# Layer norm of two token blocks together: two column sums side by side in the TensorE array, results spread through DRAM

## The chip, the cores and the metric

The kernel runs on one core of a Trainium2 chip. The metric is the device time of one execution in microseconds (us). The kernel before takes 2467.66 us, the median of 4 runs (2467.39 to 2468.02).

## The reference

The program is a stack of four layers on a tensor x of 4 batches, 512 channels and 32 x 32 = 1024 tokens, all in float32. Layer 0 is an attention with 8 heads, layer 1 a linear attention, layer 2 a layer norm with an attention of one head, layer 3 a group norm with an attention of 4 heads. Each layer adds its result to x. The change lies in the norm of layer 2:

```python
xf = jnp.transpose(x, (0, 2, 3, 1)).reshape(b, h * w, c)      # c = 512
mu = jnp.mean(xf, axis=-1, keepdims=True)
var = jnp.var(xf, axis=-1, keepdims=True)
xn = (xf - mu) * jax.lax.rsqrt(var + 1e-5) * norm_w
qkv = jnp.einsum('bnc,dc->bnd', xn, w_qkv) + b_qkv
attn = softmax(einsum('bqc,bkc->bqk', q, k) * c ** (-0.5))
out = einsum('bqk,bkc->bqc', attn, v)
return x + out @ w_proj.T + b_proj                            # and back to b, c, h, w
```

## The kernel before

**Data.** A batch of x stays in SBUF for the whole program as `xs[b]`: 128 partitions, NC = 4 chunks of 128 channels, 1024 tokens. Tokens are worked on in NTB = 2 blocks of TB = 512. So a channel is a partition in one of four chunks, a token is a column, and a sum over the 512 channels of a token is a sum of four chunks and then a sum down the 128 partitions. The second part is done on TensorE, as a matmul with a matrix of ones. Names: `ones` is 128 x 128; `eps` holds 1e-5; `row` (L89) hands out tiles of 128 x 512, five of them in all; `block` (L85) hands out tiles of four chunks by 512, twelve in all; `tr_tile` hands out one of two PSUM banks for small sums and projections. `sc_tile` and `acc_tile` are the banks of the large products, two of each. All loads, and the writes to DRAM that matter here, are issued from SyncE (SP), in one queue.

**The norm.** `layer_norm(b, dst)` (L797) takes the two token blocks one after the other. For a block, `total` (L804) has VectorE add the four chunks into a tile `part` (L812), and TensorE multiply `part` by all of `ones` (L814): every one of the 128 output rows is the same sum, so the bank `lnsum` holds the total, already copied to each partition. VectorE then computes x - mean for the four chunks (L821), reading the bank; ScalarE squares them (L828); `total` is called a second time on the squares; ScalarE takes the square root of variance + eps (L834), VectorE the reciprocal (L835), and VectorE scales the four chunks by it and by the weight `nw2` (L838). That makes two totals a block, four a batch, 16 in all.

**The order of work.** A norm is a generator. It stands in a list `background`, and `slot()` (L159), which the product loops call between their groups of matmuls, advances it by one `yield`; `later(ticks, f)` (L169) defers a step by so many slots in the same manner, and `finish()` (L176) empties the list. The order so written is not the last word: a scheduler fixes the order of the instructions of each engine when the program is built. Each engine then works through its list in that order.

- Batch 0's norm is started by `start_norm` (L888, called at L924) ahead of layer 0's attention for the last batch, and its steps are placed among the groups of that attention. There a step of `Attention.scores` (L505) is two matmuls into the halves of a bank (L517), an exponential on ScalarE (L528) and, on VectorE, the running sum of the exponentials (L532 for the first, L536). `values` (L544) multiplies the exponentials by v (L554) and copies the result out (L562). After the steps of two heads the sums go to the softmax denominators, and the result, which stands in the tiles of q by then, is multiplied by their reciprocals `rb` (L598).
- Layer 2's loop (L1005) runs over the four batches. It begins with two large products of the normed input: `channels_first` (L1012) gives q, and `tokens_first` gives v, into which VectorE adds parts of products (L356). The products go through `two_by_sevens` (L297 to L320): seven block products in the place of eight, each two groups of matmuls (L312), with VectorE forming the differences of the factors and adding the parts up, and a `slot()` after each pair of groups. After `tokens_first` the next batch's norm is started (L1028), for b = 3 a group norm; so the norms of batches 1 to 3 run among the scores (put L1041, add L1045, exponential L1048) and the values of the batch before.
- Between scores and values of layer 2, VectorE forms the softmax sums `sum0` and `sum1` and the factors `t1` (L1078), `t2` (L1087) and `t4` (L1088). The results are put and added at L1097 and L1102; the addition to x (L1107) follows a multiplication by `rb` (L1105). Weights for the next batch are loaded by `load_folded` (L967, 1 MB a transfer).

**The form that sums of several columns already use.** `spread_reciprocals` (L453) takes up to four partial sums. Each is multiplied by 32 columns of `ones` (L460), so that its total appears on 32 of the 128 partitions of one bank, `den`: four such products occupy the four quarters of the array's columns. One reciprocal (L471) serves all of them. One row of each quarter is written to a tile in DRAM (L473), and `send` reads it back, repeated on all 128 partitions, into `rb` (L589 in layer 0, L1082 in layer 2) or `dens`. Layer 0's denominators and those of layer 2's softmax go this way. `check` (L449, L995) computes bounds for a range check; the fallback that hangs on it is not executed for these inputs.

Of the kernel before, what the change touches and what calls it, by code (L numbers as in the profile page):

```python
# [12 lines left out]
F32 = mybir.dt.float32  # L13
AF = mybir.ActivationFunctionType
ALU = mybir.AluOpType
AX = mybir.AxisListType

P = 128
B = 4
C = 512  # L20
S = 1024
NC = C // P
NT = S // P
TB = 512
NTB = S // TB
# [32 lines left out]
def conv_fast(ctx: ExitStack, tc: tile.TileContext, d: dict, out: bass.AP, flag):  # L58
# [5 lines left out]
    nc = tc.nc  # L64
# [3 lines left out]
    work = ctx.enter_context(tc.tile_pool(name="work", bufs=1))  # L68
    small = ctx.enter_context(tc.tile_pool(name="small", bufs=2))
    PSUM = bass.MemoryType.PSUM  # L70
    dram = ctx.enter_context(tc.tile_pool(name="dram", bufs=1, space=bass.MemoryType.DRAM))
# [10 lines left out]
    def tr_tile(name="tr"):  # L82
        return ps_tr.tile([P, TB], F32, tag="tr", name=name)

    def block(name):  # L85

        return work.tile([P, NC, TB], F32, tag="blk", bufs=12, name=name)

    def row(name):  # L89
        return work.tile([P, TB], F32, tag="row", bufs=5, name=name)  # L90
# [5 lines left out]
    xs = [xpool.tile([P, NC, S], F32, tag=f"x{b}", name=f"x{b}") for b in range(B)]  # L96
# [29 lines left out]
    ones = const.tile([P, P], F32, name="ones")  # L126
    nc.vector.memset(ones, 1.0)
    eps = const.tile([P, 1], F32, name="eps")
# [21 lines left out]
    def col(name, c):  # L150
        return cols[:, COL[name] + c : COL[name] + c + 1]
# [125 lines left out]
    def right(xb, tiles, over=False):  # L277


        b11, b21 = xb[0][:, :HC, :], xb[0][:, HC:, :]  # L280
        b12, b22 = xb[1][:, :HC, :], xb[1][:, HC:, :]
        tt = nc.vector.tensor_tensor
        t3, t2, t4 = (tiles[i]() for i in range(3))
        t1 = b12 if over else tiles[3]()
        tt(t3, b22, b12, ALU.subtract)
        tt(t1, b12, b11, ALU.subtract)
        tt(t2, b22, t1, ALU.subtract)
        tt(t4, b21, t2, ALU.subtract)
        return {1: b11, 2: b21, 3: b22, 4: t4, 5: t1, 6: t2, 7: t3}
# [160 lines left out]
            den, den, 0.0, r, ALU.add, ALU.add, accum_out=next_unit(den.partition_size())  # L450
        )

    def spread_reciprocals(sums, send, check):  # L453


        ps = tr_tile("den")
        Q = P // 4

        def product_of(j):
            return nc.tensor.matmul(  # L460
                ps[j * Q : (j + 1) * Q, :], lhsT=ones[:, :Q], rhs=sums[j], start=True, stop=True
            )


        first = product_of(len(sums) - 1)
        with tc.issue_after(first.ins):
            for j in range(len(sums) - 1):
                product_of(j)
        n = len(sums) * Q
        r = work.tile([P, TB], F32, tag="r", bufs=1, name="r")  # L470
        nc.vector.reciprocal(r[:n, :], ps[:n, :])  # L471
        row_of = dram.tile([4, TB], F32, tag="recip", bufs=2, name="recip")
        nc.sync.dma_start(row_of[: len(sums), :], r[:n:Q, :])  # L473
        send(row_of)
        check(ps[:n, :], r[:n, :])

    class Attention:

# [100 lines left out]
        def normalize_four(s, qb, gs, to):  # L579
            sums = [s.sums.pop((qb, g)) for g in gs]  # L580
            if s.pair:
                to = spare_tile("rb")
                sums = [t[:, half, :] for t in sums for half in range(2)]

            def send(rows):
                if s.pair:
                    for half in range(2):
                        p = slice(half * s.hd, (half + 1) * s.hd)
                        nc.sync.dma_start(to[p, :, :], rows[half::2, :].partition_broadcast(s.hd))  # L589
                else:  # L590
                    n = len(sums)
                    nc.sync.dma_start(to[:, :n, :], rows[:n, :].partition_broadcast(P))

            spread_reciprocals(sums, send, check_range)

            def multiply():
                o = s.q[qb][:, gs[0] : gs[-1] + 1, :]
                nc.vector.tensor_tensor(o, o, to[:, : len(gs), :], ALU.mult)  # L598
                if s.last and qb < NTB - 1:
                    later(1, lambda: s.project_out(qb))  # L600

            later(2 if s.by > 2 else 3, multiply)
# [193 lines left out]

    def layer_norm(b, dst):  # L797

        for tb in range(NTB):
            x = xs[b][:, :, bass.ts(tb, TB)]  # L800
            xn = block("ln")
            dst.append(xn)

            def total(of):  # L804

                part = row("part")
                for c in range(NC):
                    a = of(c)
                    if c == 0:
                        first = a  # L810
                    else:
                        nc.vector.tensor_tensor(part, first if c == 1 else part, a, ALU.add)  # L812
                ps = tr_tile("lnsum")
                nc.tensor.matmul(ps, lhsT=ones, rhs=part, start=True, stop=True)  # L814
                return ps

            yield
            mean = total(lambda c: x[:, c, :])
            yield
            for c in range(NC):  # L820
                nc.vector.scalar_tensor_tensor(  # L821
                    xn[:, c, :], mean, -1.0 / C, x[:, c, :], ALU.mult, ALU.add
                )
            yield

            def square(c):
                sq = row("sq")
                nc.scalar.activation(sq, xn[:, c, :], AF.Square)  # L828
                return sq

            var = total(square)
            yield
            rstd = row("rstd")
            nc.scalar.activation(rstd, var, AF.Sqrt, bias=eps, scale=1.0 / C)  # L834
            nc.vector.reciprocal(rstd, rstd)  # L835
            yield
            for c in range(NC):
                nc.vector.scalar_tensor_tensor(  # L838
                    xn[:, c, :], xn[:, c, :], col("nw2", c), rstd, ALU.mult, ALU.mult
                )  # L840
            yield

# [58 lines left out]
    for b in range(B):  # L901
        xb = [xs[b][:, :, bass.ts(tb, TB)] for tb in range(NTB)]
        if b == 0:
            q = first_q(w0[0], "bqkv0", xb)
            x = right(xb, [pt_tile] * 4)
# [17 lines left out]
        if b == B - 1:  # L923
            start_norm(layer_norm, 0, "ln0")  # L924
            rawk = load("rawk", d["wraw2"], 1)
            rawq = load("rawq", d["wraw2"], 0)
        else:
            loads.start("q")
        att = Attention(
            b, q, k, v, 8, None, eb, then=lambda b=b: linear_attention(b),  # L930
# [73 lines left out]
    scale = float(C) ** -0.5  # L1004
    for b in range(B):  # L1005
        xn = norms.pop(f"ln{b}")
        x = right(xn, [pt_tile] * 4)
# [19 lines left out]
        if b + 1 < B:  # L1027
            start_norm(layer_norm, b + 1, f"ln{b + 1}")  # L1028
        else:
            start_norm(group_norm, 0, "gn0")  # L1030
# [50 lines left out]
        def send(rows):  # L1081
            nc.sync.dma_start(rb, rows[:2, :].partition_broadcast(P))  # L1082

        later(1, lambda: spread_reciprocals([sum0[:, 0, :], sum1[:, 0, :]], send, check_spread))

        def last_factors():
# [49 lines left out]
    total = small.tile([P, 1], F32, tag="ks", name="total")  # L1136
    nc.vector.tensor_reduce(total, stat, AX.X, ALU.add)
    ps = tr_tile("flag")
# [484 lines left out]
```

## Time and profile before

| | us |
|---|---|
| median of 4 runs | 2467.66 |
| profiled execution | 2467.66 |
| its span (first to last instruction) | 2465.7 |
| TensorE busy (PE) | 2451.8 (99%) |
| TensorE weight loads (PEld, beside matmuls) | 1148.9 (47%) |
| VectorE busy (DVE) | 1429.2 (58%) |
| ScalarE busy (ACT) | 785.5 (32%) |
| GpSimd busy (POOL) | 2.1 |
| mean DMA rate | 55 GB/s |

The clock that TensorE was granted is 1.00 over the span. By stage, in us of the span:

| stretch | what runs | PE busy | DVE busy | ACT busy |
|---|---|---|---|---|
| 0 to 956 | layer 0, with layer 1 and batch 0's norm among it | 949.4 | 623.9 | 377.6 |
| 956 to 1003 | folding of layer 2's weights | 47.0 | 36.3 | 5.6 |
| 1003 to 1622 | layer 2, with the norms of batches 1 to 3 | 617.8 | 414.8 | 177.1 |
| 1622 to 2465.7 | layer 3 | 837.7 | 354.2 | 225.3 |

The groups of the norm (instructions, busy time, mean of one):

| line | engine | what | count | busy us | mean ns |
|---|---|---|---|---|---|
| L812 | DVE | adds of x, and of squares | 16 + 16 | 11.0 + 11.0 | 688 |
| L814 | PE | total, 128 x 128 by 128 x 512 | 32 | 16.8 | 605 |
| L821 | DVE | x - mean | 32 | 20.1 | 681 |
| L828 | ACT | squares | 32 | 18.9 | 627 |
| L834 | ACT | table load ahead of the square root | 8 | 10.3 | 1283 |
| L835 | DVE | reciprocal | 8 | 26.7 | 3340 |
| L838 | DVE | scaling | 32 | 22.4 | 743 |

How to read it: a float32 matmul of the program shows as two records, so L814's 16 totals are 32. The busy time of a group is less than count times mean where ends overlap, since matmuls are pipelined and their ends are modelled; the distance between the starts of two neighbours is what one of them costs the engine. A timeline line gives the start in us, the length of the group of like instructions, engine, line, operation, output and inputs; what stands in brackets at its end is idle time ahead of it, and what ended that. In the list of waits, the numbers after the colon are the idle us, how often, and the longest.

### The profile page before, as it was taken

To read this page: it belongs to the slowest core of one execution; us is meant where nothing else is said; L and a number is where in the kernel's file an instruction comes from. 1 tells how busy PE (TensorE), PEld (TensorE's weight loads), DVE (VectorE), ACT (ScalarE), POOL (GpSimd) and SP (SyncE) were. 2 spreads that over 40 slices of the span, in tenths; PEclk is the share of its full clock that TensorE was granted. 3 is DMA by queue.
4 is the path that set the end of the run, shared out by engine and by line. 5 is a ranking of instruction groups with operands and counts; after the bars stand their busy time and mean duration, and the time that the engine had idled before them with its cause. 6 is when DMAs were issued, how large, how long until landed. Compare 5 with 4: busy or idle time off the path is not lost.

```text
span 2465.7 us, 19958 instructions
## 1 busy us (share of the span) xinstructions
PE 2451.8 (99%) x7730; PEld 1148.9 (47%) x7730; DVE 1429.2 (58%) x1732; ACT 785.5 (32%) x1120; POOL 2.1 (0%) x12
## 2 busy tenths in 40 slices
PE   9999999999999999999999999999999999999999
PEld 4534543454345334554645546446446445544643
DVE  3576567656765887568587673733553443444344
ACT  1452345135513651342241412213312321331231
POOL 0000000000000000000000000000000000000000
PEclk9999999999999999999999999999999999999999
DMA  6203100310131003002112020210031022013001
GB/s 239 94 18 120 35 1 18 120 35 1 26 112 35 9 14 114 35 0 94 52 41 100 7 76 1 77 51 18 17 137 51 1 103 102 1 52 119 18 18 44
DMA packets 44224, 135.80 MB, mean 55 GB/s; under 512 B 3446, under 2 KB 3958, under 8 KB 36572
## 3 DMA queue, kind: packets, MB, share of 16 engines
q1 hardware_dynamic: 41820, 130.28, 15.3%
q10 hardware_dynamic: 2304, 4.20, 0.5%
q8 instruction: 62, 1.02, 0.2%
q14 instruction: 38, 0.31, 0.0%
HBM read 113.28 MB, written 21.18 MB: 55 GB/s over the span
## 4 chain that ended last, share of the span: by engine, by line
PE 97%; DVE 2%; ACT 0%; issue 0%; DMA 0%; SPq 0%; DVEq 0%
PE sc L312 30%; PE acc L312 22%; PE acc L554 18%; PE sc L517 16%; PE acc L517 2%; PE acc L206 1%; PE sc L206 1%; PE z L683 1%; PE den L460 1%; PE wval L786 1%; PE kx L729 1%; PE xtr L719 1%; PE po L206 1%; PE kv L206 1%; PE lnsum L814 0%; DVE sum L536 0%
## 5 line engine op out<-in xcount | busy, mean ns | idle before, releaser
L517 PE MATMUL sc<-q,k 64*128 64x512 f32 (+1 forms) x1284 | 421.6, 601 | 1.0 <-ACT ptt L528 0.8
L554 PE MATMUL acc<-ptt,v 128*64 128x512 f32 (+1 forms) x992 | 307.7, 598 | 0.0
L528 ACT ACTIVATE ptt<-sc 128x1024 f32<-128x1024 f32 x215 | 214.5, 1026 | 219.4 <-PE sc L517 219.1
L517 PEld LDWEIGHTS sc<-q,k 64*128 64x128 f32 (+1 forms) x1284 | 165.4, 188 | 231.2 <-issue 194.0
L536 DVE TENSOR_TENSOR sum<-sum,ptt 128x1024 f32<-128x1024 f32 x144 | 176.2, 1224 | 104.9 <-ACT ptt L528 97.3
L554 PEld LDWEIGHTS acc<-ptt,v 128*64 128x64 f32 (+1 forms) x992 | 107.9, 155 | 185.9 <-issue 184.8
L536 DVE TENSOR_TENSOR sum<-sum,p 128x1024 f32<-128x1024 f32 x112 | 137.1, 1224 | 61.5 <-ACT p L528 46.8
L554 PE MATMUL acc<-p,v 128*64 128x512 f32 (+1 forms) x544 | 159.5, 596 | 0.0
L528 ACT ACTIVATE p<-sc 128x1024 f32<-128x1024 f32 x106 | 106.8, 1037 | 95.4 <-PE sc L517 95.4
L352 ACT COPY v<-sc 128x256 f32<-128x256 f32 x144 | 53.6, 372 | 224.8 <-PE sc L312 222.6
L333 ACT ACTIVATE k<-sc,cols 128x512 f32<-128x512 f32 x48 | 33.0, 687 | 263.2 <-PE sc L312 263.2
L471 DVE RECIPROCAL r<-den 128x512 f32<-128x512 f32 (+1 forms) x28 | 94.0, 3356 | 36.8 <-PE den L460 36.3
L532 DVE TENSOR_TENSOR sum<-ptt 128x1024 f32<-128x1024 f32 x52 | 63.6, 1223 | 86.7 <-ACT ptt L528 77.8
L554 PEld LDWEIGHTS acc<-p,v 128*64 128x64 f32 (+1 forms) x544 | 56.1, 152 | 97.0 <-issue 97.0
L312 PE MATMUL acc<-ptt,ws 128*128 128x512 f32 x224 | 101.2, 592 | 0.0
L356 DVE TENSOR_TENSOR v<-acc,v 128x256 f32<-128x256 f32 x144 | 55.5, 418 | 68.2 <-PE acc L312 60.7
L562 ACT COPY q<-acc 128x512 f32<-128x512 f32 x64 | 37.6, 587 | 160.5 <-PE acc L554 160.5
L312 PE MATMUL sc<-ptt,w 128*128 128x512 f32 x168 | 75.5, 592 | 0.0
L337 DVE TENSOR_TENSOR k<-acc,k 128x512 f32<-128x512 f32 x48 | 31.6, 687 | 66.5 <-PE acc L312 66.5
L312 PEld LDWEIGHTS acc<-ptt,ws 128*128 128x128 f32 x224 | 42.3, 190 | 52.1 <-issue 52.1
L517 PE MATMUL acc<-q,k 64*128 64x512 f32 x252 | 66.1, 601 | 0.0
L333 ACT ACTIVATE q<-sc,cols 128x512 f32<-128x512 f32 x42 | 28.9, 688 | 109.1 <-PE sc L312 109.1
(356 smaller groups left out, 3481.4 us busy)
## 6 DMA issues: line engine op xcount, KB each, us to landing
ws<-kept SPq DMA_DIRECT2D x28, 1024.0 KB, 4.8
w<-in_wqkv SPq DMA_DIRECT2D x24, 1024.0 KB, 6.1
kept<-wsum SPq DMA_DIRECT2D x8, 1024.0 KB
rb<-recip SPq DMA_DIRECT2D x32, 256.0 KB, 4.1
w<-in_wo SPq DMA_DIRECT2D x7, 1024.0 KB, 5.9
dens<-recip SPq DMA_DIRECT2D x7, 1024.0 KB, 4.6
x<-in_x SPq DMA_DIRECT2D x3, 2048.0 KB
wqk<-kept SPq DMA_DIRECT2D x6, 1024.0 KB, 5.0
```

Of the source, the lines that this page charges most:

```text
L206: nc.tensor.matmul(ps, lhsT=lhs(c), rhs=rhs(c), start=(c == 0), stop=(c == NC - 1))
L312: nc.tensor.matmul(ps, lhsT=lhs, rhs=rhs, start=not more and j == 0, stop=(j == pieces - 1), skip_group_check=more,)
L333: nc.scalar.activation(out[at[1]][:, o, :], ps, AF.Identity, bias=bias(o))
L352: nc.scalar.copy(at_block(which, at), ps)
L356: nc.vector.tensor_tensor(c, ps, c, ALU.add)
L471: nc.vector.reciprocal(r[:n, :], ps[:n, :])
L517: nc.tensor.matmul(ps[half], lhsT=s.k[key // QT][p0:p1, g, bass.ts(key % QT, P)], rhs=s.q[qb][p0:p1, g, :], start=True, stop=True,)
L528: nc.scalar.activation(pt, pair_of, AF.Exp, scale=s.scale)
L532: nc.vector.tensor_tensor(t, s.pts[i - 1], pt, ALU.add)
L536: nc.vector.tensor_tensor(t, t, pt, ALU.add)
L554: nc.tensor.matmul(ps[p0:p1, :], lhsT=s.v[key // QT][:, key % QT, g * P + p0 : g * P + p1], rhs=pt[:, half, :], start=(key == 0), stop=(ke ...
L562: nc.scalar.copy(s.q[qb][:, g, :], s.accs.pop((qb, g)))
```

## The change

The norm handles both token blocks of a batch at once and takes over the form of `spread_reciprocals`, which is split into `column_totals` (the products into quarters) and `rows_of` (the write of one row of each quarter to DRAM). For each batch:

- VectorE adds up the chunks of both blocks into two tiles `part`. One `column_totals` of the two gives both sums, each on 32 partitions of one bank.
- ScalarE scales the bank by -1/C into a tile `total` of 64 partitions, two rows of it go to DRAM, and two transfers bring each row back, repeated on 128 partitions, as `lnrow` tiles: the negated means.
- After two `yield`s, VectorE adds the means to x, now a `tensor_tensor` of two SBUF tiles instead of a `scalar_tensor_tensor` that reads PSUM.
- Squares and their adds are as before. One `column_totals` gives both variances; one square root and one reciprocal on 64 partitions serve both blocks, and two rows go through DRAM to `lnrow` tiles in the same way.
- After two more `yield`s, VectorE scales all chunks of both blocks.

For a batch that makes two pairs of 128 x 32 products in the place of four 128 x 128 products, one table load, one square root and one reciprocal in the place of two each, one added scaling on ScalarE and six added transfers (two writes of two rows, four reads of 256 KB). The steps between the `yield`s are fewer and larger.

```diff
@@ -450,8 +450,7 @@
             den, den, 0.0, r, ALU.add, ALU.add, accum_out=next_unit(den.partition_size())
         )
 
-    def spread_reciprocals(sums, send, check):
-
+    def column_totals(sums):
 
         ps = tr_tile("den")
         Q = P // 4
@@ -466,13 +465,22 @@
         with tc.issue_after(first.ins):
             for j in range(len(sums) - 1):
                 product_of(j)
-        n = len(sums) * Q
-        r = work.tile([P, TB], F32, tag="r", bufs=1, name="r")
-        nc.vector.reciprocal(r[:n, :], ps[:n, :])
-        row_of = dram.tile([4, TB], F32, tag="recip", bufs=2, name="recip")
-        nc.sync.dma_start(row_of[: len(sums), :], r[:n:Q, :])
-        send(row_of)
-        check(ps[:n, :], r[:n, :])
+        return ps[: len(sums) * Q, :]
+
+    def rows_of(t):
+
+        n = t.partition_size()
+        rows = dram.tile([4, TB], F32, tag="recip", bufs=2, name="recip")
+        nc.sync.dma_start(rows[: n * 4 // P, :], t[:: P // 4, :])
+        return rows
+
+    def spread_reciprocals(sums, send, check):
+
+        ps = column_totals(sums)
+        r = work.tile([P, TB], F32, tag="r", bufs=1, name="r")[: ps.partition_size(), :]
+        nc.vector.reciprocal(r, ps)
+        send(rows_of(r))
+        check(ps, r)
 
     class Attention:
 
@@ -796,47 +804,65 @@
 
     def layer_norm(b, dst):
 
-        for tb in range(NTB):
-            x = xs[b][:, :, bass.ts(tb, TB)]
-            xn = block("ln")
-            dst.append(xn)
-
-            def total(of):
-
-                part = row("part")
-                for c in range(NC):
-                    a = of(c)
-                    if c == 0:
-                        first = a
-                    else:
-                        nc.vector.tensor_tensor(part, first if c == 1 else part, a, ALU.add)
-                ps = tr_tile("lnsum")
-                nc.tensor.matmul(ps, lhsT=ones, rhs=part, start=True, stop=True)
-                return ps
-
+
+        blocks = range(NTB)
+        xb = [xs[b][:, :, bass.ts(tb, TB)] for tb in blocks]
+        xn = [block("ln") for _ in blocks]
+        dst.extend(xn)
+
+        def partial(of):
+
+            part = row("part")
+            for c in range(NC):
+                a = of(c)
+                if c == 0:
+                    first = a
+                else:
+                    nc.vector.tensor_tensor(part, first if c == 1 else part, a, ALU.add)
+            return part
+
+        def spread(t):
+            rows = rows_of(t)
+            to = [row("lnrow") for _ in blocks]
+            for tb in blocks:
+                nc.sync.dma_start(to[tb], rows[tb : tb + 1, :].partition_broadcast(P))
+            return to
+
+        parts = []
+        for tb in blocks:
             yield
-            mean = total(lambda c: x[:, c, :])
+            parts.append(partial(lambda c: xb[tb][:, c, :]))
+        yield
+        ps = column_totals(parts)
+        t = row("total")[: ps.partition_size(), :]
+        nc.scalar.activation(t, ps, AF.Copy, scale=-1.0 / C)
+        mean = spread(t)
+        yield
+        yield
+        parts = []
+        for tb in blocks:
+            for c in range(NC):
+                nc.vector.tensor_tensor(xn[tb][:, c, :], mean[tb], xb[tb][:, c, :], ALU.add)
             yield
+
+            def square(c):
+                sq = row("sq")
+                nc.scalar.activation(sq, xn[tb][:, c, :], AF.Square)
+                return sq
+
+            parts.append(partial(square))
+            yield
+        ps = column_totals(parts)
+        t = row("total")[: ps.partition_size(), :]
+        nc.scalar.activation(t, ps, AF.Sqrt, bias=eps[: ps.partition_size(), :], scale=1.0 / C)
+        nc.vector.reciprocal(t, t)
+        rstd = spread(t)
+        yield
+        yield
+        for tb in blocks:
             for c in range(NC):
                 nc.vector.scalar_tensor_tensor(
-                    xn[:, c, :], mean, -1.0 / C, x[:, c, :], ALU.mult, ALU.add
-                )
-            yield
-
-            def square(c):
-                sq = row("sq")
-                nc.scalar.activation(sq, xn[:, c, :], AF.Square)
-                return sq
-
-            var = total(square)
-            yield
-            rstd = row("rstd")
-            nc.scalar.activation(rstd, var, AF.Sqrt, bias=eps, scale=1.0 / C)
-            nc.vector.reciprocal(rstd, rstd)
-            yield
-            for c in range(NC):
-                nc.vector.scalar_tensor_tensor(
-                    xn[:, c, :], xn[:, c, :], col("nw2", c), rstd, ALU.mult, ALU.mult
+                    xn[tb][:, c, :], xn[tb][:, c, :], col("nw2", c), rstd[tb], ALU.mult, ALU.mult
                 )
             yield
```

## The prediction

> **What bounds the kernel now.** I read the page, the waits of TensorE, and then timelines around the two kinds of column sum.
>
> ```profile
> PE 2451.8 (99%) x7730; PEld 1148.9 (47%) x7730; DVE 1429.2 (58%) x1732; ACT 785.5 (32%) x1120; POOL 2.1 (0%) x12
> PE sc L206 <- DMA wq<-in_wqkv: 5.7, 1, 5.7
> PE acc L312 <- DVE v L356: 0.9, 1, 0.9
> PE sc L517 <- ACT ptt L528: 0.8, 2, 0.6
> ```
>
> TensorE (PE) works for all of the span; its waits after the start come to 2 us. So time is won only where TensorE gets less work, and lost where another engine now makes it wait. Idle VectorE or ScalarE time is worth nothing by itself.
>
> The totals to be replaced, in layer 2 (start, length, records):
>
> ```profile
> 1074.71 3.60 PE L312 MATMUL acc<-q,ln 128*128 128x512 f32 x8
> 1078.15 1.02 PE L814 MATMUL lnsum<-part,ones 128*128 128x512 f32 x2
> 1079.01 3.60 PE L312 MATMUL sc<-rq,ptt 128*128 128x512 f32 x8
> ```
>
> A float32 matmul is two records 0.43 us apart. Starts count, since ends overlap: one total costs 1079.01 - 1078.15 = 0.86 us. The two-sum form exists already, for layer 2's softmax:
>
> ```profile
> 1133.94 1.88 PE L312 MATMUL acc<-p,v 128*128 128x512 f32 x4
> 1135.75 1.05 PE L460 MATMUL den<-sum,ones 128*32 128x512 f32 x4
> 1136.73 1.13 PE L312 MATMUL acc<-p,v 128*128 128x512 f32 x2
> 1137.69 0.59 PE L312 MATMUL sc<-t,sv 128*128 128x512 f32 x1
> ```
>
> Before it, four records fill TensorE to 1135.66; after it, two fill 0.86 ahead of 1137.69, from 1136.83. The pair costs 1.17 us, against 1.72 for two totals.
>
> What spreading through DRAM takes is seen in layer 0:
>
> ```profile
> 885.71 3.36 DVE L471 RECIPROCAL r<-den 128x512 f32<-128x512 f32 x1
> 889.10 0.53 SPq L473 DMA_DIRECT2D recip<-r  x1
> 890.87 1.24 SPq L589 DMA_DIRECT2D rb<-recip  x2
> 895.99 1.23 DVE L598 TENSOR_TENSOR q<-q,rb 128x1024 f32<-128x1024 f32 x1 [1.45 <-DMA rb<-recip]
> ```
>
> The reader may leave 1.77 us after the write; both 256 KB rows have landed 6.9 us after the write was issued. The second read leaves 0.65 later than the first; rb landings have a median of 4.0 us, so I take 5.9 us for the first row.
>
> The last view, ScalarE in layer 0's last attention, shows how norm work gets into the way of the softmax:
>
> ```profile
> 846.31 1.00 ACT L528 ACTIVATE ptt<-sc 128x1024 f32<-128x1024 f32 x1
> 847.22 1.14 ACT L828 ACTIVATE sq<-ln 128x512 f32<-128x512 f32 x2
> 848.26 1.01 ACT L528 ACTIVATE ptt<-sc 128x1024 f32<-128x1024 f32 x1
> 849.32 1.13 PE L517 MATMUL sc<-q,k 64*128 64x512 f32 x4 [0.58 <-ACT ptt L528]
> ```
>
> Squares stand between two exponentials, and TensorE, which needs the bank that the second one frees, waits.
>
> **What the Trainium skill says.** "TensorEngine Tiling (Array Packing)", Key Properties: tiles of the array work in parallel, but a change of mode drains it. The trace agrees: a pair costs 0.31 more than one total. "TensorE: Matmul & The Clock Gate", Architectural detail: ScalarE's and VectorE's queues are strict FIFO; the last view agrees. "DMA: Bandwidth & Descriptors", Anatomy of one DMA: about 2 us of a transfer is fixed, mostly the receipt of the write; 1.77 here. "ScalarE: Activation LUTs", What ACT_TABLE_LOAD costs: 1.28 us; the table loads at L834 take 1.28.
>
> **The change, part by part.** The profiled execution took 2467.66 us (span 2465.7 and 2.0 around it), the same as the median.
>
> (1) TensorE's work. Layer 2 computes the norms of batches 1 to 3: 12 totals x 0.86 = 10.3 become 6 pairs x 1.17 = 7.0: -3.3. Batch 0's norm runs in layer 0's last attention, where a total costs 1.05 (817.56 to 818.61): 4.2. Its first pair stands between attention groups: the four-sum den there costs 1.00 (884.58 to 885.58), two sums at least 0.88 and at most 1.17; I take 1.00. In the built order its second pair follows a softmax den in the same mode: two record steps of 0.44, 0.88. So -2.3.
>
> (2) Waits on `v`. Two first totals stand ahead of matmuls that wait for VectorE's adds (L356): 0.9 in the list, 0.2 in a gap (1354.8 to 1355.07). A pair that is 0.31 longer uses up 0.3 and 0.2 of them: -0.5 (bounds 0 and -1.1).
>
> (3) VectorE and ScalarE. 8 reciprocals of 3.34 become 4; 8 scalings by ScalarE stay 8 (0.69); 8 table loads go; the 32 subtractions keep 0.68 (L812's tensor_tensor: 0.69). This is hidden by TensorE before and after: 0, except in (4) and (5).
>
> (4) Batch 0: a new wait. VectorE's subtraction waits for the mean rows; behind it wait the running sums (L536). ScalarE's squares wait for the subtraction; behind those stand exponentials, and behind these TensorE. Put together from the rows: the value group ahead of the pair starts 1.05 + 0.4 earlier than 824.71 (the first total and a wait for its squares are gone), ends at 825.1; pair to 826.1; score and value groups (1.91, 1.87) follow, and the score group after two of each is due at 833.7. Sums are visible 1.13 after a pair's start (884.58 to 885.71): 826.3; scaling 0.69: 827.0; rows at 832.9 and 833.8. The first subtraction ends at 833.6. In the order built, two squares precede the exponential of the score group of 829.9: they run 833.7 to 834.9, the exponential to 835.9. The group due at 833.7 starts at 836.0: +2.3. Its second half waits for another square and exponential: +0.5. The second block's squares alternate with exponentials likewise, each behind subtractions (0.6) that stand among sums (1.13): the next two score groups get their second and first half 1.2 late each. Sum 5.2; the waits that today's squares cause at 822.4 and 847.6 go (groups of 2.31 and 2.77 for 1.91): -1.3. Net +3.9; bounds 0 (rows early) and 7 (rows 3 us later).
>
> (5) Layer 2: is there room? Clock from the variance pair's start. Sums visible 1.1, table load 1.28, square root 0.69, reciprocal 3.35, handovers: 6.6. Row at 12.5, second at 13.4. Eight scalings at 0.66: 17.8; four adds `p<-acc` (0.6): 20.2. TensorE needs the second add's bank at 1.17 + 6 groups x 3.43 = 21.8: 2.7 to spare. Next on VectorE, from the rows of 1124 to 1137: 12.7 us of sums and differences until the softmax sums are ready, 32.9. TensorE comes there at 21.8 + 6.9 + 5.1 = 33.8: 0.9 to spare; for the differences `t2` and `t4` 1.5 each. So 0, but this cover is thin: past 0.9 us, each us of lateness costs one in each of three batches. The mean rows have more room: in batches 2 and 3 they are ordered some 35 us ahead of use, in batch 1 about 3 us. Order moves as well: the softmax pair goes six matmuls later, t2 ahead of its reciprocal; late next is the division by `rb`, whose waiter (a score bank of the next stage) has 2 us. Taken 0, bounds 0 and +7.
>
> (6) SP issues 24 more transfers (8 writes, 16 reads of 256 KB, 0.5 to 0.65 each). Batch 0's variance rows follow softmax rows, whose write and reads are out by then. In layer 2 the rows go ahead of the folded weights' loads, needed 30 us later; the first `wvo` load now precedes the softmax rows, but leaves before their reciprocal ends. 0.
>
> Sum: -3.3 - 2.3 - 0.5 + 3.9 = -2.2, so 2465.5 us.
>
> **The rivals.** *A, the above*: most of the gain is paid back in layer 0; own range 2463.3 to 2468. Chance 0.67. *B, rows are hidden everywhere*: -6.1, 2461.5 us. For: ScalarE has slack of 1.8 us per group at 836 and 840. Against: 5.9 us is longer than that. 0.18. *C, VectorE stands on rows that come late* (slower). Place: the scalings by rstd in layer 2 and the first subtraction in layer 0. With 1 MB loads ahead, writes gave way to reads after 2.8 and 3.2 us (1140.22 to 1142.99, 1585.76 to 1588.96), and two rb landings took 5.8: together 3.1 late. Then +3.1 in batch 0 and 3 x (3.1 - 0.9) = 6.6: +7.5, 2475.2 us. It is level with before from 1.2 us of lateness. Against: in the built order no 1 MB load is ahead of these rows. 0.12. *D, the two sums don't share the array*: 4 records x 0.43 + 0.31 = 2.0 for a pair, 8 x 0.86 = 6.9 more than A: 2472.4. Against: the den pair above. 0.03.
>
> **How the numbers follow.** The likeliest case gives 2465.5. To hold 8 in 10 I go down to B with a little of (2), 2461.2, and up to 2470.5, where rows are about 1.2 us late in all batches; C and D stay out. A measurement of this kernel tells about 0.2%, 4.9 us, from no change. Faster by that is B and A's tail, 0.19; slower is C and part of D, 0.13; within, 0.68.
>
> **What would show it.** Right: 32 den<-part records, pairs 1.2 us apart in layer 2; VectorE's first subtraction by lnrow in layer 0 idle on the DMA at about 833; near 836 to 847 a few TensorE waits on ScalarE's exponentials, 5 us together; none of weight in layer 2. Wrong: no such waits (B), or TensorE waiting at `acc<-p,v` or at the softmax pair behind scalings that wait for lnrow (C), or pairs of 2 us (D).

## The result, and the profile after

The changed kernel takes 2465.35 us, the median of 40 runs (2464.35 to 2466.59); the kernel before takes 2468.02 in 60 runs that were made beside it (2466.99 to 2469.19). The ratio is 0.9989, with a 95% interval from 0.9985 to 0.9994. So the change wins 2.7 us, 0.1%, where 2.2 was forecast; the interval, 1.5 to 3.7 us below before, holds both. The profiled execution has a span of 2464.2.

The engines' busy times, from its page:

```profile
PE 2447.0 (99%) x7730; PEld 1144.3 (46%) x7730; DVE 1414.0 (57%) x1728; ACT 774.4 (31%) x1112; POOL 2.1 (0%) x12
```

VectorE has 15.2 less to do (four reciprocals of 3.34 are 13.4 of it) and ScalarE 11.1 less (eight table loads of 1.28 are 10.2). The time does not follow them.

The waits of TensorE in the changed kernel (line numbers move: L517 is now L525, L528 is L536, L460 is L459):

```profile
PE sc L206 <- DMA wq<-in_wqkv: 5.7, 1, 5.7
PE sc L525 <- ACT ptt L536: 4.4, 6, 1.3
PE acc L312 <- DVE v L356: 0.8, 1, 0.8
```

One row has changed much: the wait for ScalarE's exponentials has grown from 0.8 to 4.4. Layer 2 has no new wait: the one on `v`, 0.9 before and 0.8 now, stands in it, and none on the additions into p or on the softmax sums. The list counts idle time up to the modelled ends of matmuls; what a wait costs in all is read from starts, below.

I matched the same matmuls in the two traces and took the difference of their starts. It says where the time went:

| stretch of the trace before | shift at its end (after less before) | change in the stretch |
|---|---|---|
| start to 800 (the first weights land later in this execution) | +0.65 | +0.65 |
| layer 0's last attention, with batch 0's norm | +2.31 | +1.66 |
| layer 2, batch 0 (with the norm of batch 1) | +1.24 | -1.07 |
| batch 1 (with the norm of batch 2) | -0.16 | -1.40 |
| batch 2 (with the norm of batch 3) | -1.56 | -1.40 |

The first row has nothing to do with the change. The rest is -2.2: layer 2 wins 3.9, layer 0 loses 1.7. In the batches that win 1.40, and not 1.07, the first sum stands ahead of a wait on `v`. In the kernel before, in batch 1:

```profile
1199.51 3.62 PE L312 MATMUL sc<-wvo,ptt 128*128 128x256 f32 x16
1202.97 1.02 PE L814 MATMUL lnsum<-part,ones 128*128 128x512 f32 x2
1204.88 2.43 PE L312 MATMUL acc<-wvo,ptt 128*128 128x256 f32 x10 [0.89 <-DVE v L356]
```

From 1199.51 to 1204.88 are 5.37 us; in the changed kernel, with a pair in the place of the total, the same way (1200.75 to 1206.12) takes 5.37 too. The dearer pair costs nothing there, as the wait takes it up.

What layer 2 wins, on TensorE's timeline of the changed kernel:

```profile
1105.67 3.60 PE L312 MATMUL sc<-rq,ptt 128*128 128x512 f32 x8
1109.19 1.05 PE L459 MATMUL den<-part,ones 128*32 128x512 f32 x4
1110.18 3.70 PE L312 MATMUL acc<-rq,ptt 128*128 128x512 f32 x8
1113.71 3.60 PE L312 MATMUL sc<-rq,ln 128*128 128x512 f32 x8
```

From 1105.67 to 1113.71 are 8.04 us. Two undisturbed groups of eight records take 2 x 3.43 (1098.80 to 1102.23, for one). So the pair costs 1.18, as the softmax's pair did; some 0.1 of it lies ahead of it and 0.1 behind, and two totals before cost 1.72.

What layer 0 loses, on ScalarE's and then on TensorE's timeline:

```profile
833.67 1.23 ACT L850 ACTIVATE sq<-ln 128x512 f32<-128x512 f32 x2 [2.25 <-DVE ln L845]
834.80 1.01 ACT L536 ACTIVATE ptt<-sc 128x1024 f32<-128x1024 f32 x1
835.71 0.62 ACT L850 ACTIVATE sq<-ln 128x512 f32<-128x512 f32 x1
836.23 1.01 ACT L536 ACTIVATE ptt<-sc 128x1024 f32<-128x1024 f32 x1
```

```profile
835.86 1.13 PE L525 MATMUL sc<-q,k 64*128 64x512 f32 x4 [1.30 <-ACT ptt L536]
837.30 1.13 PE L525 MATMUL sc<-q,k 64*128 64x512 f32 x4 [0.30 <-ACT ptt L536]
...
842.60 1.13 PE L525 MATMUL sc<-q,k 64*128 64x512 f32 x4 [1.25 <-ACT ptt L536]
...
846.48 2.04 PE L525 MATMUL sc<-q,k 64*128 64x512 f32 x8 [0.89 <-ACT ptt L536]
```

ScalarE is idle for 2.25 us in front of two squares, and the exponential at 834.80 stands behind them. Its scores begin at 830.71; in the group before, 1.17 us lie between the scores and the exponential (826.93 to 828.10), so it could have started at about 831.9. The squares wait for VectorE's subtraction (L845), and VectorE waits for the mean row:

```profile
832.94 2.50 DVE L845 TENSOR_TENSOR ln<-lnrow,x 128x512 f32<-128x512 f32 x4 [1.65 <-DMA lnrow<-recip]
```

The four waits of TensorE come to 3.74 in the list. By the starts they cost 4.5: a score group and a value group take 1.91 and 1.87 us, and what lies beyond these between 832.63 and 848.46 is 4.5. A fifth wait, 0.38 in the list and 0.7 by the starts, is at 880; one of 0.27 at 814 was there before. A further 0.17 is lost at 809, where VectorE now adds up both blocks ahead of layer 1's last additions.

### The profile page after: what moved, and what is told of

Its sections match the earlier page's. It is cut to its first block, busy times and chain, and to the rows that moved or that the text cites. A ratio compares the mean times of both kernels' runs of the same rounds, so it can differ in the third digit from the quotient of the medians.

```text
span 2464.2 us, 20001 instructions
## 1 busy us (share of the span) xinstructions
PE 2447.0 (99%) x7730; PEld 1144.3 (46%) x7730; DVE 1414.0 (57%) x1728; ACT 774.4 (31%) x1112; POOL 2.1 (0%) x12
## 4 chain that ended last, share of the span: by engine, by line
PE 97%; DVE 2%; issue 0%; DMA 0%; ACT 0%; SPq 0%; DVEq 0%; ACTq 0%
PE sc L312 30%; PE acc L312 23%; PE acc L562 18%; PE sc L525 15%; PE acc L525 2%; PE acc L206 1%; PE den L459 1%; PE sc L206 1%; PE z L691 1%; PE wval L794 1%; PE kx L737 1%; PE xtr L727 1%; PE po L206 1%; PE kv L206 1%; DVE sum L544 0%
## 5 line engine op out<-in xcount | busy, mean ns | idle before, releaser
L525 PE MATMUL sc<-q,k 64*128 64x512 f32 (+1 forms) x1284 | 422.0, 602 | 4.4 <-ACT ptt L536 4.4
L536 ACT ACTIVATE ptt<-sc 128x1024 f32<-128x1024 f32 x215 | 214.6, 1026 | 221.5 <-PE sc L525 214.0
L525 PEld LDWEIGHTS sc<-q,k 64*128 64x128 f32 (+1 forms) x1284 | 165.2, 188 | 235.5 <-issue 193.1
L536 ACT ACTIVATE p<-sc 128x1024 f32<-128x1024 f32 x106 | 106.8, 1038 | 95.4 <-PE sc L525 95.4
L525 PE MATMUL acc<-q,k 64*128 64x512 f32 x252 | 66.1, 601 | 0.0
```

The lines of the kernel that those rows point to most:

```text
L525: nc.tensor.matmul(ps[half], lhsT=s.k[key // QT][p0:p1, g, bass.ts(key % QT, P)], rhs=s.q[qb][p0:p1, g, :], start=True, stop=True,)
L536: nc.scalar.activation(pt, pair_of, AF.Exp, scale=s.scale)
```

## The experiments

All were timed beside the kernel before. The interval is that of the ratio.

| kernel | median, us | ratio to before, interval | expected |
|---|---|---|---|
| changed kernel | 2465.35 | 0.9989 (0.9985 to 0.9994) | 2465.5 |
| e1_layer2_only | 2464.14 | 0.9983 (0.9976 to 0.9990) | 2464.2 |
| e2_batch0_only | 2469.80 | 1.0007 (0.9998 to 1.0015) | 2469.6 |
| e4_whole_array | 2467.72 | 0.9998 (0.9989 to 1.0006) | 2467.5 to 2468.0 |
| e3_order_batch0 | 2463.47 | 0.9982 (0.9975 to 0.9990) | 2461 to 2462 |
| e7_order_and_scaling | 2461.45 | 0.9975 (0.9965 to 0.9984) | 2461 to 2462 |
| e6_late_rows | 2478.73 | 1.0045 (1.0031 to 1.0060) | 2473 to 2480 |
| e5_four_sums | 2474.94 | 1.0027 (1.0016 to 1.0038) | 2457 to 2459 |
| e8_four_sums_scaling | 2467.66 | 1.0000 (0.9992 to 1.0008) | 2457 or less |
| e9_best | 2462.27 | 0.9974 (0.9965 to 0.9984) | 2457 to 2458 |

### The two places apart: e1 and e2

The theory is the prediction's sum by place; the rivals share the 2.7 us out in other ways. `layer_norm_alone` is the norm as it was before.

```diff
-            start_norm(layer_norm, 0, "ln0")              # e1
+            start_norm(layer_norm_alone, 0, "ln0")
```

```diff
-            start_norm(layer_norm, b + 1, f"ln{b + 1}")   # e2
+            start_norm(layer_norm_alone, b + 1, f"ln{b + 1}")
```

> The norms of batches 1 to 3 (layer 2) as in the changed kernel, batch 0's norm as before. Theory (the prediction's sum by place): layer 2 is worth -3.3 - 0.5, so 3.8 below the kernel before, 2464.2; no TensorE wait on exponentials beyond the 0.8 of before. Rival 1 (batch 0 costs nothing, so that layer 2 alone makes the whole difference): 2.7 below, 2465.3. Rival 2 (layer 2 has lost part of its gain and batch 0 has won): 2466 or more.

> Batch 0's norm as in the changed kernel, the norms of batches 1 to 3 as before. Theory: -2.3 of TensorE's work and +3.9 of waits for the mean rows, so 1.6 above the kernel before, 2469.6, with 4 to 5 us of TensorE waits on exponentials between 834 and 847. Rival 1: 0 (2468.0), no such waits. Rival 2: -2.3 (2465.7).

The change in layer 2 alone gives 3.9 less than before (2468.07 in these rounds), the change in batch 0 alone 1.7 more. The interval of the second takes in no change, so its sign is not sure from the times; the trace says more. TensorE's waits in e1, and then in e2:

```profile
PE sc L525 <- ACT ptt L536: 0.8, 2, 0.6
```

```profile
PE sc L525 <- ACT ptt L536: 4.3, 6, 1.3
```

The row follows batch 0's norm. The times alone do not part the theory from the first rival (the interval of e1 holds 2465.3). The matched starts do: in e1 layer 2's batches win 3.9 (1.07, 1.39 and 1.40) and layer 0 nothing; in e2 layer 0 loses 1.5 and layer 2 nothing. Both rivals are out.

### Is it the shared array? e4

An excerpt, against the changed kernel:

```diff
-        ps = column_totals(parts)
-        t = row("total")[: ps.partition_size(), :]
-        nc.scalar.activation(t, ps, AF.Copy, scale=-1.0 / C)
-        mean = spread(t)
+        mean = [row("lnrow") for _ in blocks]
+        for tb in blocks:
+            nc.scalar.activation(mean[tb], whole(parts[tb]), AF.Copy, scale=-1.0 / C)
```

`whole` is the old product with all of `ones`; the square root is treated alike, with a reciprocal for each block.

> In layer 2 both token blocks go together as in the changed kernel, but each sum has the whole array to itself (the old 128 x 128 product, 0.86 us), and ScalarE copies its bank to a row: no quarters and no way through DRAM. Batch 0 as before. Theory (the gain in layer 2 is the shared array): at most the 0.5 of the waits on v are left, 2467.5 to 2468.0, 3.3 above the kernel that has the change in layer 2 alone. Rival (handling both blocks at once, with fewer table loads and reciprocals and another order, is what pays): 2464.2 as there.

It came out at 2467.72, 0.35 below before and 3.6 above e1. So handling both blocks at once, with half of the table loads at the square root in layer 2, brings nothing that can be measured. The kernel e4 has as many reciprocals as before, so it doesn't try these; but the matched starts of e1 put all of the gain at the places of the sums (0.54 for each pair, and what the waits on `v` take up). The quarters bring it.

### Is it the order on ScalarE? e3

The scheduler had put the squares up to two groups of the attention ahead of where the program writes them, and so in front of exponentials. Here they must stay behind, and the subtractions behind a running sum (an excerpt):

```diff
+        def behind(engine):
+            return tc.issue_after(latest[engine].ins) if b == 0 else ExitStack()
...
-            for c in range(NC):
-                nc.vector.tensor_tensor(xn[tb][:, c, :], mean[tb], xb[tb][:, c, :], ALU.add)
+            with behind("sum"):
+                for c in range(NC):
+                    nc.vector.tensor_tensor(xn[tb][:, c, :], mean[tb], xb[tb][:, c, :], ALU.add)
...
-            parts.append(partial(square))
+            with behind("exp"):
+                parts.append(partial(square))
```

> The changed kernel, but in batch 0's norm the subtractions stand behind the running sum, and the squares behind the exponential, that were traced before them; the scheduler had put them one to two groups earlier. Nothing is left out. Theory (TensorE waits because squares that wait for the mean rows stand ahead of exponentials): the waits of 4.4 us fall to under 1, so 3.5 to 4.4 below the changed kernel, 2461 to 2462. Rival (the 4.4 us are what 8 squares and 8 subtractions cost wherever they stand, since ScalarE has no room there): waits of 3 us or more stay, 2464 or more.

It gained 1.9 on the changed kernel, half of what was expected. The orders of ScalarE and VectorE were changed together; which of the two counts was not tried apart. In the stretch itself the theory holds: one wait of 0.47 at 841.75 is left of the four. But others came up further on. TensorE, and then VectorE, in e3:

```profile
855.78 2.04 PE L526 MATMUL sc<-q,k 64*128 64x512 f32 x8 [0.70 <-ACT ptt L537]
...
871.86 2.04 PE L526 MATMUL sc<-q,k 64*128 64x512 f32 x8 [0.82 <-ACT ptt L537]
...
877.44 1.13 PE L526 MATMUL sc<-q,k 64*128 64x512 f32 x4 [0.61 <-ACT ptt L537]
```

```profile
852.51 3.35 DVE L482 RECIPROCAL r<-den 128x512 f32<-128x512 f32 x1
855.77 3.29 DVE L864 RECIPROCAL total<-total 64x512 f32<-64x512 f32 x1
...
866.82 2.73 DVE L870 SCALAR_TENSOR_TENSOR ln<-ln,cols,lnrow 128x512 f32<-128x512 f32 x4
869.47 1.22 DVE L541 TENSOR_TENSOR sum<-ptt 128x1024 f32<-128x1024 f32 x1
870.61 2.73 DVE L870 SCALAR_TENSOR_TENSOR ln<-ln,cols,lnrow 128x512 f32<-128x512 f32 x4
```

No bracket with idle time stands in VectorE's lines from 850 until 895.96: it is busy for 43.5 of 44.6 us, up to 894.6. The exponentials then wait for its running sums, whose inputs are the tiles that they write next. That would mean that the waits at 836 to 847 had given VectorE the time to keep up, and that with them gone VectorE is what is late. The next kernel tries it.

### VectorE's backlog: e7

Batch 0's scalings are needed by layer 2 only, and VectorE has idle time after 898. They were put nine slots later, on top of e3 (an excerpt):

```diff
-        yield
-        yield
+        for _ in range(11 if b == 0 else 2):
+            yield
         for tb in blocks:
-            for c in range(NC):
+            with behind("sum"):
+                for c in range(NC):
```

> The kernel with subtractions and squares of batch 0 put later, and in addition batch 0's eight scalings (5.4 us of VectorE) put behind running sums nine slots later, where VectorE has idle time. Theory (half of what the order won was taken back because VectorE works without a gap from 850 to 880): TensorE's waits on exponentials fall from 2.9 to under 1.2, about 2 below the kernel with the order alone, 2461 to 2462. Rival (the waits at 855 to 877 come from the table loads and the reciprocals alone): 2463 to 2463.5, waits of 2.5 or more.

2461.45, as expected, with this row in place of 2.9 (e3) and 4.4 (changed kernel):

```profile
PE sc L526 <- ACT ptt L537: 1.4, 3, 0.7
```

So the 1.9 and the 2.0 are the two halves of what the waits of batch 0's norm cost: the order on ScalarE and VectorE, and behind it the work on VectorE. The 0.70 at 855, ahead of which the two table loads stand, is still there (855.51 in e7), so the rival had that part right. This version is 3.9 below the changed kernel and 6.4 below before (2467.9 in its rounds).

### How much room do the rows have in layer 2? e6

An excerpt:

```diff
+            for _ in range(hops):
+                then = dram.tile([4, TB], F32, tag="hop", bufs=4, name="hop")
+                nc.sync.dma_start(then[:NTB, :], rows[:NTB, :])
+                rows = then
...
-        rstd = spread(t)
+        rstd = spread(t, 3 if b else 0)
```

The additions into p that follow were held behind the scalings, as they stand in the changed kernel. That hold was not run without the hops.

> The changed kernel, but in layer 2 the two variance rows pass three further tiles in DRAM before they are spread, and the additions into p from the banks stand behind the scalings that wait for the rows, as in the changed kernel. Theory (the rows' time is hidden by 2.7 us of room at the banks of p and no more): with three hops of 1.8 to 2.5 us the rows are 5.4 to 7.5 later, TensorE waits for the additions into p 2.7 to 4.8 in each of three batches, so 8 to 14 above the changed kernel, 2473 to 2480. Rival (the rows have far more room than was worked out, or the scheduler's other order hides them): 2465 to 2468.

Three hops took 5.9 us (the spreading read leaves at 1123.42, in the changed kernel at 1117.48). TensorE then waited:

```profile
PE acc L313 <- DVE p L1077: 6.4, 3, 2.8
...
PE den L460 <- DVE sum L1108: 3.8, 2, 1.9
```

In the norm of batch 1 the first scaling is 6.1 late (1127.07 for 1120.98) and the wait at the bank of p is 2.76. By the starts it costs 2.9, so there were some 3.3 us of room, where 2.7 had been worked out. The softmax pair comes next, in the other two batches: there the first scaling is 5.3 late, beside what TensorE is late by then, and TensorE loses 4.0 in all, so the room was 1.3, where 0.9 had been worked out. Both places named in step (5) are where late rows are paid. The loss of 13 us is more than the waits in the list, 10.2, though: after 2.76 us of idle time TensorE is slow for a while, of which more below.

### A further step that failed: e5, e8 and e9

If two sums share the array at the price of 1.18, four might. With the sums of x and of its squares taken together, the variance is the mean of squares less the square of the mean, and one way through DRAM serves both (an excerpt):

```diff
+        nc.scalar.activation(t[:H, :], ps[:H, :], AF.Copy, scale=-1.0 / C)
+        nc.scalar.activation(m2[H:, :], ps[:H, :], AF.Square, scale=1.0 / C)
+        nc.vector.scalar_tensor_tensor(
+            t[H:, :], ps[H:, :], 1.0 / C, m2[H:, :], ALU.mult, ALU.subtract
+        )
+        nc.scalar.activation(t[H:, :], t[H:, :], AF.Sqrt, bias=eps[H:, :])
+        nc.vector.reciprocal(t[H:, :], t[H:, :])
+        rows = rows_of(t)
```

> Sums of x and of x squared of both blocks (four) go through the array at once; the variance is the mean of squares less the square of the mean, so one way through DRAM brings mean and rstd rows, and no square waits for a row. Theory: TensorE has one four-sum of about 1.2 us in the place of two pairs of 1.17 in each of three batches (-3.4) and one of 1.0 in batch 0 (-0.9); of batch 0's waits 2 to 4 us go, as VectorE, full from 850 on, allows: 6.3 to 8.3 below the changed kernel, 2457 to 2459. Rival (VectorE or ScalarE give it back: squares now stand in the stretch before the sums, and the chain of variance, root and reciprocal is longer): 2462 or more.

> The kernel with four sums at once, and batch 0's scalings put nine slots later. Theory: whatever TensorE still waits for exponentials in batch 0 with the four sums goes, to under 1.2 us in all; 4.3 of work and 3.4 or more of waits below the changed kernel, 2457 or less. Rival (VectorE's backlog isn't the scalings): no difference from the four sums alone.

The four-sum itself costs what was thought: matched against the changed kernel, taking out a pair moves TensorE by -1.18, and the four-sum moves it by +1.19. The rest was wrong; the rival of e5 describes it. The squares of x need nothing but x, so the scheduler starts them early, in front of the attention's first exponentials, where they wait for VectorE. TensorE's waits in e5:

```profile
PE sc L525 <- ACT ptt L536: 8.1, 4, 3.3
...
PE acc L312 <- DVE v L356: 1.8, 2, 1.0
```

The first of these waits is behind a square that waits for VectorE. ScalarE, then TensorE, in e5:

```profile
814.02 0.63 ACT L834 ACTIVATE sq<-x 128x512 f32<-128x512 f32 x1 [1.96 <-DVE part L836]
...
815.96 1.02 ACT L536 ACTIVATE ptt<-sc 128x1024 f32<-128x1024 f32 x1
```

```profile
817.04 3.78 PE L525 MATMUL sc<-q,k 64*128 64x512 f32 x8 [3.01 <-ACT ptt L536]
820.75 3.00 PE L562 MATMUL acc<-ptt,v 128*64 128x512 f32 x8
```

Putting subtractions and scalings behind running sums, and the scalings later (e8), wins 7.3 us, since together they had filled VectorE from 853 to 864; 3.9 of the row stay, 3.0 of them at 817, where the squares are. (The matched traces give 5.8: the profiled execution of e8 is one of the five of 13 that took 2469.0 or more, while the others took 2467.8 or less.) So e8 stays 10 us above its expectation, and the rival of e8, no difference, is out as well. In e9, batch 0 is as in e7, and layer 2's four sums stand behind the last step of v:

```diff
+            with behind("v_add"):
+                parts.append(partial(lambda c: xb[tb][:, c, :]))
```

> Batch 0's norm with two pairs, its subtractions, squares and scalings put later; in layer 2 four sums at once, with all their adds and squares put behind the last step of v, where the kernel with four sums had lost time. Theory (four sums cost TensorE as much as two, 1.2 us; what the four sums lost was squares ahead of exponentials in batch 0 and norm steps ahead of those of v): three times 1.2 less than the kernel with order and scaling put later, and 0.8 of waits on v gone, 2457 to 2458. Rival (the four sums, ready later now, make the rows late for the additions into p or for the softmax sums): 2461 or more, with waits of TensorE on VectorE there.

2462.27: no gain on e7. The norm of batch 1 wins 1.2 in the matched traces, 0.4 of it ahead of its sums. Those of batches 2 and 3 lose 0.5 each. In the changed kernel their first pair stands where TensorE has to wait for v anyway:

```profile
1204.29 1.05 PE L459 MATMUL den<-part,ones 128*32 128x512 f32 x4
1206.12 1.13 PE L312 MATMUL acc<-wvo,ptt 128*128 128x256 f32 x4 [0.77 <-DVE v L356]
```

With the pair gone, the wait takes its place, and TensorE's row in e9 reads:

```profile
PE acc L313 <- DVE v L357: 2.7, 2, 1.8
...
PE sc L313 <- DVE p L1145: 0.6, 3, 0.2
```

The last row is the rival's place, and costs 0.35 by the starts in each of the three batches: eight subtractions and eight scalings now stand together on VectorE for 10.1 us (1104.58 to 1114.70), and the additions into p stand behind them.

That the first pair had been nearly free where TensorE waits for `v` was on record in step (2), and I had not used it: the price of a pair is 1.18 only where TensorE has no wait next to it.

## Why the prediction was right

The sum, term by term:

| step | forecast | measured | from |
|---|---|---|---|
| (1) layer 2, work of TensorE | -3.3 | -3.2 | matched starts, 3 x -1.07 |
| (2) waits on v used up | -0.5 | -0.65 | matched starts, batches 2 and 3: 2 x (1.40 - 1.07) |
| (1) and (4), batch 0 together | +1.6 | +1.66 | matched starts; e2: +1.7 |
| (3) VectorE's and ScalarE's work | 0 | 0 | matched starts: nothing is left over; e4 for the table loads |
| (5), (6) layer 2's rows and queues | 0 | 0 | no wait on them in TensorE's list |
| sum | -2.2 | -2.2 (traces), -2.7 (medians) | |

The mechanism is shown for the steps that carry the sum, not only the sum: (1) by e4 and the matched starts, (2) by the matched starts, (4) by e3, e7 and the lines at 833 to 847, (5) by e6. For (6) there is only that no such wait appears.

That batch 0 came out at +1.66 is luck in part, as errors cancel in it. By the starts, its sums cost 1.85 (pairs of 0.99 and 0.86) in place of 4.22, so -2.4 for the forecast -2.3, and today's waits of 1.3 are gone as forecast. The new waits between 834 and 847 cost 4.5, not 5.2, since the first row was in use 5.26 us after its write was issued (827.68 to 832.94), not 5.9. But 0.7 for VectorE's backlog at 880 and 0.2 for its adds at 809 were not foreseen, and they make up for the difference: the waits come to +4.1 net, where 3.9 was forecast.

One sum of the prediction is wrong, and touches only the upper end of its range. It puts 2470.5 where rows are 1.2 us late in all batches. By its own price, one us for each us in batch 0 and three for each beyond 0.9 in layer 2, rows 1.2 late give 2467.6, level with before, as its rival C says; 2470.5 takes 1.9 us.

One thing that the prediction implied was wrong, though it did not touch its number: that without the waits for the rows layer 0 would win 3.9 more, as in rival B. e3 shows that half of it is VectorE's limit, which stood behind the wait for the rows. Only e7, which moves VectorE's work as well, reaches what B promised: 6.4 below before, for 6.1.

Of the rivals, B (rows hidden everywhere) is out by the lines at 833; D by the pair of 1.18. C did not occur, and e6 shows that its mechanism is real and where its price begins.

## What to carry to other kernels

A step that is free on paper because its engine has idle time can hold that engine's queue: here what counted was not how long the squares take, but that exponentials stood behind squares that waited for a row from DRAM. Look at what the scheduler put behind the instruction that waits, and when you have moved it, look which engine is the next to have no gap; the gain is cut off there. And a price per instruction, however well measured, holds only where the engine isn't going to wait next to it anyway.

## What the runs showed of the hardware

- After an idle time of about 3 us TensorE works at half speed for a while. In e5 it waits 3.01 us up to 817.04, and then eight records take 3.71 in place of 1.91 (817.04 to 820.75). Windows of e5 (busy times of the engines, then the granted clock in the third column from the end):

```profile
817.00:820.70 3.70, 3.66 (x8) 1.13 (x8) 2.94 (x4) 2.96 (x4) 0.00 (x0) 0.50 0.00 0
820.70:824.00 3.30, 3.30 (x12) 1.07 (x12) 1.97 (x2) 1.02 (x1) 0.00 (x0) 0.66 0.00 0
```

  The clock is 0.50 and recovers within 7 us. In e6 a wait of 2.76 does the same, and so does one of 3.34 at 871 in e5: the matched starts slip by a further 1.7 and 1.5 over the next records. After the waits of 1.3 in the changed kernel, and of up to 1.9 in e6, nothing of the kind is seen. So a wait of about 3 us costs another 1.5 to 2.9 us (the 2.9 at 817: 1.8 in those eight records and 1.1 in the next eight). It isn't the longest wait that costs most: worked out from windows of 1 to 5 us, the clock is halved for 6.8 us at the 3.01 (from 0.9 us before that wait ends), and for 3.4 us at the 3.34 and the 2.76; in e6 this starts only 1.0 us after the wait has ended. The Trainium skill ("TensorE: Matmul & The Clock Gate", "HAM oscillation — how this bites in real kernels") warns of idle gaps of more than about 3.4 us; here gaps of 2.8 and 3.0 us were enough.
- Four sums of 32 columns each cost TensorE as much as two (1.19 in e9 and 1.18 us in the changed kernel, between groups that use the whole array).
- A hop of two rows of 2 KB from DRAM to DRAM took 1.9 to 2.1 us in e6, from the issue of one transfer to that of the next that waits for it.
